# A graph attention layer and a mixture of experts: both scores of a node in layer 2's table rows, and the sort's features in two halves

## The chip, the cores and the metric

The kernel runs on one core of a Trainium2 chip. The metric is device time in microseconds, the median of several runs. The engines are named as in the profile: PE multiplies matrices (PEld is its loading of weights), DVE works on vectors, ACT evaluates functions and copies, POOL issues indirect DMAs (gathers and scatters by a list of indices), and SP issues plain DMAs. SP and ACT each have a queue of their own, and every engine runs its instructions in the order written.

## The reference

There are 6250 nodes with 256 features and 206250 edges (100000 pairs in both directions, and a loop at each node). The layer norm of x goes through eight attention heads of 64 features, then through one output layer of 256, then through a mixture of eight experts of which each node takes two.

```python
def _gat_layer(x, src, dst, W, b, a, g, beta, N, concat):
    h = x @ W.T + b
    d = W.shape[0]
    s_src = h @ a[:d]
    s_dst = h @ a[d:]
    score = s_src[src] + s_dst[dst]
    e = jnp.exp(-jax.nn.leaky_relu(score, ALPHA))
    h_prime = jax.ops.segment_sum(e[:, None] * h[dst], src, num_segments=N)
    # layer norm with g and beta, then elu (heads only)
...
heads = [_gat_layer(embeds, src, dst, W_heads[i], ...) for i in range(H)]
x = jnp.concatenate(heads, axis=1)
out = _gat_layer(x, src, dst, W_out, b_out, a_out, g_out, beta_out, N, concat=False)
return jax.nn.elu(out)
...
x = x + gnn(layernorm(x))
x = x + moe(layernorm(x))
```

A node thus has two scores per head: one as a source of an edge (s_src) and one as its destination (s_dst). An edge needs the source's score of one node, and the features and the destination's score of the other.

## The kernel before

The nodes lie in 49 blocks of 128. The work has three stages.

**The sort.** All edges are sorted by the block of their source, in 23 segments. A segment goes through stages on DVE and PE (`rows_of_blocks`, `counts_before`, `places_before`, `places`, `both_sides`) and ends in `append`: PE collects what each block gets (`run_ps`, L278), ACT copies it (L281), and POOL sends it out with four scatters (L283) into the list `srt` in DRAM. A scatter writes where another has written, so each waits until the one before has landed. Between these stages, by a schedule written out by hand, `tick` does the features of layer 1, a block at a time: `normed_x` (ACT), `turned_x` (PE), `turned_copy` (ACT), `products` (PE) and `table_rows`. `products` (L357 to L364) multiplies a block of 128 nodes with the weights `wt`, which have C1 = 528 columns: 512 features, then 8 scores as destination and 8 as source. It writes the 512 features to the PSUM bank `ph` and the 16 scores to the bank `pk`. The 256 input features are two pieces of 128 (KF = 2), and each such f32 product shows as two instructions in the profile; the bias is one more product, in bf16. `table_rows` copies both banks into one row of 528 and stores 520 columns of it to layer 1's table `tab1`; the source's scores stay in SBUF (`s1`) and are written to `ssrc1` once, at the end of the sort.

**Layers 1 and 2, `edges`.** Each block has at most 34 tiles of 128 edges, in groups of five. A group is loaded, weighted and added in stages at fixed distances: `sources` (SP, L643) loads the sources' numbers, `gather` (POOL, L649) fetches for each edge of a tile the table row of its destination, one gather a tile; `one_hot` (DVE), `source_sums` (PE, L662) and `weigh` (DVE and ACT, L665) make the weights of the edges; `messages` (DVE) makes the one-hot matrix and in layer 1 the weighted rows; `add` (PE, L705) sums them into the block's nodes. The source's score comes not from a table but from `sel`, made from the scores in SBUF. Edges that did not fit a block's tiles go through `far_messages`, one tile of at most 128 for each layer: it gathers the sources' scores from `ssrc` (L624) and the rows of the destinations (L626).

After each block of layer 1, `middle` does the layer norm, the elu and the products of layer 2, and stores a row for each node. That row has 258 columns: 256 features, the score as destination, the score as source. Its first R2 = 257 columns go to the table `tab2` (L845), the last one alone to `ssrc2` (L847), 4 bytes a node, and to `s2` in SBUF (L848).

After each block of layer 2, `tail` makes the tokens, and `experts` runs in between (L1019, L1027, L1032).

**A way out.** If the sort overflows, `every_edge` does all edges one by one. It stands behind a condition on `over_i`, and none of its instructions are in this trace.

Of the kernel before, what the change touches and what calls it, by code (L numbers as in the profile page):

```python
# [23 lines left out]
F32 = mybir.dt.float32  # L24
# [7 lines left out]
P = 128  # L32
# [16 lines left out]
def kernel(ctx: ExitStack, tc: tile.TileContext, x, src, dst, w_heads, b_heads, a_heads,  # L49
                        g_heads, beta_heads, w_out, b_out, a_out, g_out, beta_out, router, w1, b1, w2, b2,  # L50
                        out):
    nc = tc.nc
    N, F = x.shape
    E = src.shape[0]
    H, D = b_heads.shape
    HD = H * D
    R1 = HD + H
    R2 = F + 1
    NE = w1.shape[0]
    KF = F // P  # L60
    KH = HD // P
# [1 line left out]
    NB = -(-N // P)  # L63
    LAST = N - (NB - 1) * P
    EP = P - 1
# [21 lines left out]
    dram = ctx.enter_context(tc.tile_pool(name="dram", bufs=1, space=bass.MemoryType.DRAM))  # L87
# [2 lines left out]
    srow = dram.tile([NB * PIT], BF16, name="srow")  # L90
    tab1 = dram.tile([NB * P + 1, R1], F32, name="tab1")
    ssrc1 = dram.tile([NB * P, H], F32, name="ssrc1")
    ssrc2 = dram.tile([NB * P, 1], F32, name="ssrc2")
    tab2 = dram.tile([NB * P + 1, R2], F32, name="tab2")

    const = ctx.enter_context(tc.tile_pool(name="const", bufs=1))
# [192 lines left out]
    C1 = HD + 2 * H  # L289
# [67 lines left out]
    def products(b):  # L357
        ph = bank("ph", "ph")
        pk = bank("pk", "pk")
        for to, cols in ((ph, slice(0, HD)), (pk[:, :2 * H], slice(HD, C1))):  # L360
            for k in range(KF):
                nc.tensor.matmul(to, blocks[b][:, k, :], wt[:, k, cols], start=(k == 0), stop=False)
            nc.tensor.matmul(to, three, bias3[:, cols], start=False, stop=True)
        blocks[b] = ph, pk  # L364

    def table_rows(b):
        ph, pk = blocks.pop(b)
        row = sw.tile([P, C1], F32, name="row", bufs=2)
        nc.scalar.copy(row[:, HD:], pk[:, :2 * H])
        nc.scalar.copy(row[:, :HD], ph)  # L370
        nc.scalar.copy(s1[:, b, :], row[:, R1:])
        nc.sync.dma_start(tab1[b * P:(b + 1) * P, :], row[:, :R1])

# [213 lines left out]
    def edges(es, layer, table, sel, ssrc, k, width, block_done, more=None):  # L587

        row = width + k
        GB = 6 if k > 1 else 8
        RB = 6
        eb = es.enter_context(tc.tile_pool(name=f"edge_b{layer}", bufs=1))
# [23 lines left out]
        def far_messages():  # L618

            if layer == 1:  # L620
                yield from read_far(eb)
                yield
            ss = eb.tile([P, k], F32, name="far_ss")
            nc.gpsimd.indirect_dma_start(out=ss, out_offset=None, in_=ssrc,  # L624
                                         in_offset=bass.IndirectOffsetOnAxis(ap=far_src, axis=0))
            nc.gpsimd.indirect_dma_start(out=far_gt, out_offset=None, in_=table,  # L626
                                         in_offset=bass.IndirectOffsetOnAxis(ap=far_dst, axis=0))
            yield
            yield
            yield  # L630
            nc.vector.tensor_scalar_mul(ss, ss, far_good)
            nc.vector.tensor_add(ss, ss, far_gt[:, width:])
            edge_weights(eb, far_ee, ss)
            yield
            if k > 1:
                hv = far_gt[:, :width].rearrange("p (h d) -> p h d", h=k)
                nc.vector.tensor_mul(hv, hv, far_ee[:, :, None].to_broadcast([P, k, width // k]))
# [27 lines left out]
        def weigh(n):  # L665
            nt = size(n)
            ssum = eb.tile([P, GT, k], F32, name="ssum", bufs=2)[:, :nt]
            nc.vector.tensor_reduce(ssum, now[n]["ps"][:, :nt * 3 * k].rearrange("p (j t k) -> p j k t", j=nt, t=3),  # L668
                                    axis=AX.X, op=OP.add)
            nc.vector.tensor_add(ssum, ssum, now[n]["gt"][:, :nt, width:])  # L670
            if k > 1:
                ee = now[n]["ee"] = bank("ee", "ee")[:, :nt * k].rearrange("p (j k) -> p j k", j=nt)
            else:
                ee = tile_of(n, "ee", [P, GT, k], 3)[:, :nt]
            edge_weights(eb, ee, ssum)
# [62 lines left out]

    def every_edge(es, layer, table, ssrc, k, width):

        row = width + k
        rows = NB * P
        EP = 125
        EC = E // EP
        assert EP * EC == E
        gd = es.enter_context(tc.tile_pool(name=f"any_d{layer}", bufs=1, space=bass.MemoryType.DRAM))
        gc = es.enter_context(tc.tile_pool(name=f"any_c{layer}", bufs=1))
        gw = es.enter_context(tc.tile_pool(name=f"any_w{layer}", bufs=1))
        sums = gd.tile([rows + P, width], F32, name=f"sums{layer}")
        zeros = gc.tile([P, width], F32, name="zeros")  # L750
        nc.vector.memset(zeros, 0.0)
        for b in range(NB + 1):
            nc.sync.dma_start(sums[b * P:(b + 1) * P, :], zeros)
        lower = gc.tile([P, P], F32, name="lower")
        nc.vector.tensor_scalar(lower, iota_n, iota_p, None, op0=OP.is_lt)
        with tc.For_i(0, EC, 1) as i:
            si = gw.tile([EP, 1], I32, name="si")
            nc.sync.dma_start(si, src.rearrange("(p c) -> p c", p=EP)[:, bass.ds(i, 1)])
            di = gw.tile([EP, 1], I32, name="di")
            nc.sync.dma_start(di, dst.rearrange("(p c) -> p c", p=EP)[:, bass.ds(i, 1)])  # L760
            gt = gw.tile([EP, row], F32, name="gt_any")
            nc.gpsimd.indirect_dma_start(out=gt, out_offset=None, in_=table,
                                         in_offset=bass.IndirectOffsetOnAxis(ap=di, axis=0))
            sg = gw.tile([EP, k], F32, name="sg")
            nc.gpsimd.indirect_dma_start(out=sg, out_offset=None, in_=ssrc,
                                         in_offset=bass.IndirectOffsetOnAxis(ap=si, axis=0))
            nc.vector.tensor_add(sg, sg, gt[:, width:])
            ee = gw.tile([EP, k], F32, name="ee_any")
            edge_weights(gw, ee, sg)
            hv = gt[:, :width].rearrange("p (h d) -> p h d", h=k)  # L770
            nc.vector.tensor_mul(hv, hv, ee[:, :, None].to_broadcast([EP, k, width // k]))

            sf = gw.tile([EP, 1], F32, name="sf")
            nc.vector.tensor_copy(sf, si)
            wide = gw.tile([EP, P], F32, name="wide")
            nc.vector.tensor_copy(wide, sf.to_broadcast([EP, P]))
            pt = bank("pt", "pt_any")
            nc.tensor.transpose(pt[:, :EP], wide, ident[:EP, :EP])
            same = gw.tile([EP, EP], F32, name="same")
            nc.vector.tensor_scalar(same, pt[:EP, :EP], sf, None, op0=OP.is_equal)  # L780
            prev = gw.tile([EP, EP], F32, name="prev")
            nc.vector.tensor_mul(prev, same, lower[:EP, :EP])
            many = gw.tile([EP, 1], F32, name="many")
            nc.vector.tensor_reduce(many, prev, axis=AX.X, op=OP.max)

            to = gw.tile([EP, 1], F32, name="to")
            nc.vector.tensor_scalar(to, iota_p[:EP], float(rows), sf, op0=OP.add, op1=OP.subtract)
            nc.vector.scalar_tensor_tensor(to, to, many, sf, op0=OP.mult, op1=OP.add)
            ti = gw.tile([EP, 1], I32, name="ti")
            nc.vector.tensor_copy(ti, to)  # L790
            acc = bank("acc", "acc_any")
            nc.tensor.matmul(acc[:EP, :width], same, gt[:, :width], start=True, stop=True)
            old = gw.tile([EP, width], F32, name="old")
            nc.gpsimd.indirect_dma_start(out=old, out_offset=None, in_=sums,
                                         in_offset=bass.IndirectOffsetOnAxis(ap=ti, axis=0))
            nc.vector.tensor_add(old, old, acc[:EP, :width])
            nc.gpsimd.indirect_dma_start(out=sums, out_offset=bass.IndirectOffsetOnAxis(ap=ti, axis=0),
                                         in_=old, in_offset=None)
        return sums


    def middle(ms):
        mw = ms.enter_context(tc.tile_pool(name="mid_w", bufs=2))

        def block_done(b, acc):
# [36 lines left out]
            yield  # L842
            row = mw.tile([P, C2], F32, name="row2")
            nc.vector.tensor_add(row, ph[:, :C2], bo)
            nc.sync.dma_start(tab2[b * P:(b + 1) * P, :], row[:, :R2])  # L845
            with nc.allow_non_contiguous_dma(reason="one element of a node"):
                nc.sync.dma_start(ssrc2[b * P:(b + 1) * P, :], row[:, R2:])  # L847
            nc.vector.tensor_copy(s2[:, b, :], row[:, R2:])  # L848
        return block_done


# [239 lines left out]
    with ExitStack() as es:  # L1091
        psum_of("second", es, acc=2, ps=2, ffn=3, pt=1)
        done, more = tail(es)
        edges(es, 2, tab2, sel2, ssrc2, 1, F, done, more)


    with tc.If(nc.values_load(over_i[:1, :1], min_val=0, max_val=1) > 0):
# [9 lines left out]
                    pass  # L1107
        with ExitStack() as es:
            psum_of("second_any", es, acc=1, pt=2, ffn=3)
            sums = every_edge(es, 2, tab2, ssrc2, 1, F)  # L1110
            done, more = tail(es)
            bw = es.enter_context(tc.tile_pool(name="back2", bufs=2))
            for b in range(NB):
# [47 lines left out]
```

## Time and profile before

| | |
|---|---|
| median of 3 runs | 5668.95 us (5641.82 to 5675.06) |
| the profiled execution, its own time | 5686.65 us |
| its span | 5684.9 us |
| mean granted clock of PE | 0.834 |

By stage, in us of busy time, read from the busy times of each engine in stretches of the span:

| stretch | what | PE | DVE | ACT | POOL | DMA share |
|---|---|---|---|---|---|---|
| 0 to 429 | sort and features | 342.69 | 372.85 | 96.94 | 178.68 | 0.21 |
| 429 to 3108 | layer 1 | 1944.62 | 1725.45 | 378.37 | 1600.21 | 0.70 |
| 3108 to 5550 | layer 2 with experts | 1771.68 | 1137.96 | 794.19 | 1611.89 | 0.45 |
| 5550 to 5685 | last experts | 116.95 | 52.48 | 40.19 | 0.00 | 0.04 |

The profile is of one execution. A line of its answers in order of time has the start in us, the duration in us, the engine, the line of the kernel, the operation, what it writes and reads, how many alike follow each other, and in brackets how long the engine was idle before and what ended that. A group's line has the busy time, the mean of one in ns, and the idle time before with its releasers. PE's matmuls overlap, so that one's duration is longer than the distance to the next; distances are read from the starts. The releaser is inferred, and where an instruction waits for several things it can be the wrong one.

### The profile page before, as it was taken

Reading aid. Unit: us, or ns where it says so; the run is one execution under the profiler, and the core shown is the slowest. Engines: PE = TensorE matmul, PEld = TensorE weight load, DVE = VectorE, ACT = ScalarE, POOL = GpSimd, SP = SyncE. Lnnn points to the kernel's source line nnn. Section 1 sums busy time; section 2 is a strip of 40 time slices with the busy share of each in tenths; the row PEclk is TensorE's granted clock in tenths of the full one; section 3 lists DMA queues with packets and bytes.
Section 4 is the critical chain, followed back from the end, with each engine's and each line's share of the span. In section 5 each row is a group of like instructions: output and inputs, shape, how many; then the busy total and the mean of one; then the engine's idle time right before and its main releaser. Section 6 shows DMA issues by size and latency. Waiting matters only on the chain.

```text
span 5684.9 us, 52631 instructions
## 1 busy us (share of the span) xinstructions
PE 4175.9 (73%) x16462; PEld 2477.2 (44%) x16462; DVE 3288.7 (58%) x8048; ACT 1309.7 (23%) x2440; POOL 3390.8 (60%) x3450
## 2 busy tenths in 40 slices
PE   5984777777777777777776447777778777777778
PEld 4762333333333333333333335555555555545556
DVE  9975666666666666666666334454444445444444
ACT  1220111111111111111111113333334333333433
POOL 3446656665666666666554666666666666666660
PEclk8996878888888888888778668888888888888989
DMA  2216767786677777777665544444444444444440
GB/s 69 66 51 186 196 187 188 195 210 182 195 192 186 201 190 194 190 195 191 184 189 141 141 118 111 122 119 113 119 122 112 121 120 120 113 119 122 112 112 14
DMA packets 378008, 825.33 MB, mean 145 GB/s; under 512 B 91759, under 2 KB 210779, under 8 KB 377718
## 3 DMA queue, kind: packets, MB, share of 16 engines
q0 software_dynamic: 216464, 665.03, 44.0%
q1 hardware_dynamic: 155868, 151.02, 9.5%
q10 hardware_dynamic: 5386, 5.83, 0.3%
q8 instruction: 131, 2.15, 0.2%
q14 instruction: 159, 1.30, 0.1%
HBM read 792.59 MB, written 28.99 MB: 145 GB/s over the span
## 4 chain that ended last, share of the span: by engine, by line
PE 35%; DVE 26%; issue 17%; another core or an unknown queue 12%; POOL 7%; DMA 2%; DVEq 0%; ACT 0%; POOLq 0%; ACTq 0%; SPq 0%
PE acc L705 18%; DVE msg L687 10%; POOL gt L649 7%; PE ph L1019 6%; PE py L1027 6%; DVE hot L684 2%; DMA gt<-tab,dst_idx 2%; DVE hot L693 1%; DVE ot L656 1%; PE run_ps L278 1%; PE ps L662 1%; DVE ssum L670 1%; DVE ssum L668 1%; DVE what L266 1%
## 5 line engine op out<-in xcount | busy, mean ns | idle before, releaser
L649 POOL DMA_INDIRECT gt<-tab,dst_idx x3324 | 3206.4, 965 | 1908.4 <-issue 923.3
L705 PE MATMUL acc<-msg,hot 128*128 128x512 f32 x3324 | 1711.6, 659 | 180.4 <-issue 178.6
L705 PE MATMUL acc<-gt,hot 128*128 128x256 f32 x3324 | 1004.0, 445 | 176.2 <-issue 167.8
L705 PEld LDWEIGHTS acc<-msg,hot 128*128 128x128 f32 x3324 | 666.4, 209 | 944.5 <-issue 942.9
L687 DVE TENSOR_TENSOR msg<-gt,ee 128x2560 f32<-128x2560 f32 (+1 forms) x342 | 935.2, 2735 | 0.0
L705 PEld LDWEIGHTS acc<-gt,hot 128*128 128x128 f32 x3324 | 697.7, 219 | 337.1 <-issue 230.5
L585 ACT ACTIVATE ee<-lr 128x40 f32<-128x40 f32 (+3 forms) x684 | 141.7, 207 | 2348.7 <-DVE lr L584 1250.0
L662 PE MATMUL ps<-sel,ot 128*128 128x24 bf16 (+1 forms) x3324 | 204.4, 171 | 649.7 <-issue 314.8
L693 DVE TENSOR_SCALAR hot<-iota_n,sloc,ee 128x128 f32<-128x128 f32 x1662 | 461.6, 357 | 330.9 <-remote 166.6
L684 DVE TENSOR_TENSOR hot<-iota_ps,sloc 128x640 f32<-128x640 f32 (+1 forms) x342 | 273.4, 799 | 603.8 <-remote 514.2
L662 PEld LDWEIGHTS <-ot 128*128 128x128 bf16 x3324 | 192.3, 100 | 945.5 <-issue 707.0
L1032 DVE SCALAR_TENSOR_TENSOR xq<-py,comb,xq 128x256 f32<-128x256 f32 x392 | 171.0, 478 | 577.2 <-remote 162.5
L1027 PE MATMUL py<-w2s,h 128*128 128x256 f32 x1568 | 410.5, 402 | 57.9 <-issue 52.9
L1019 PE MATMUL ph<-tokt,w1s 128*128 128x512 f32 (+1 forms) x832 | 408.0, 618 | 25.1 <-issue 23.6
L585 ACT ACT_TABLE_LOAD x252 | 323.3, 1283 | 375.8 <-DVE lr L584 178.6
L1027 PEld LDWEIGHTS py<-w2s,h 128*128 128x128 f32 x1568 | 312.2, 203 | 149.9 <-issue 99.9
L283 POOL DMA_INDIRECT srt<-run,to x92 | 168.4, 1830 | 247.9 <-DMA srt<-run,to 148.8
L668 DVE TENSOR_REDUCE ssum<-ps 128x40 f32<-128x120 f32 (+3 forms) x684 | 149.6, 219 | 252.8 <-remote 197.4
L656 DVE TENSOR_SCALAR ot<-rb,iota_p 128x640 bf16<-128x640 bf16 (+1 forms) x684 | 259.0, 379 | 7.2 <-DMA rb<-srow 7.2
L1019 PEld LDWEIGHTS ph<-tokt,w1s 128*128 128x128 f32 x832 | 162.4, 206 | 168.1 <-issue 157.9
L1021 ACT ACTIVATE h<-ph,b1s 128x512 f32<-128x512 f32 (+1 forms) x208 | 135.5, 662 | 368.1 <-remote 210.1
L840 PE MATMUL ph<-wo,ht 128*128 128x258 f32 x392 | 126.1, 476 | 84.8 <-DVE ht L837 79.1
(248 smaller groups left out, 3248.6 us busy)
## 6 DMA issues: line engine op xcount, KB each, us to landing
rb<-srow SPq DMA_DIRECT2D x588, 160.0 KB
gt<-tab,dst_idx POOLq DMA_INDIRECT x3324
tab<-row SPq DMA_DIRECT2D x49, 260.0 KB
rb<-srow SPq DMA_DIRECT2D x96, 128.0 KB
tab<-row SPq DMA_DIRECT2D x49, 128.5 KB
xq<-in_x_dram SPq DMA_DIRECT2D x12, 512.0 KB
out_dram<-xq SPq DMA_DIRECT2D x12, 512.0 KB
xc<-in_x_dram SPq DMA_DIRECT2D x6, 896.0 KB
```

The costliest lines, as they stand in the source:

```text
L585: nc.scalar.activation(ee, lr, AF.Exp, scale=-1.0)
L649: nc.gpsimd.indirect_dma_start(out=gt[:, j, :], out_offset=None, in_=table, in_offset=bass.IndirectOffsetOnAxis(ap=dst_idx[c][:, t0 + j:t0 ...
L656: nc.vector.tensor_scalar(ot[:, :cols], now[n]["rb"][:, :cols], iota_p, None, op0=OP.is_equal)
L662: nc.tensor.matmul(ps[:, j * 3 * k:(j + 1) * 3 * k], ot[:, j * P:(j + 1) * P], sel[:, groups[n][0]].rearrange("p t k -> p (t k)"), start=T ...
L668: nc.vector.tensor_reduce(ssum, now[n]["ps"][:, :nt * 3 * k].rearrange("p (j t k) -> p j k t", j=nt, t=3), axis=AX.X, op=OP.add)
L684: nc.vector.tensor_tensor(hot, iota_ps[:, None, :P].to_broadcast([P, nt, P]), sl[:, :, None].to_broadcast([P, nt, P]), op=OP.is_equal)
L687: nc.vector.tensor_mul(msg.rearrange("p j (h d) -> p j h d", h=k), gt[:, :, :width].rearrange("p j (h d) -> p j h d", h=k), ee[:, :, :, No ...
L693: nc.vector.tensor_scalar(hot[:, j, :], iota_n, sl[:, j:j + 1], ee[:, j, :], op0=OP.is_equal, op1=OP.mult)
L705: nc.tensor.matmul(accs[b][:, :width], now[n]["hot"][:, j, :], now[n]["msg"][:, j, :width], start=(g == 0 and j == 0), stop=False)
L1019: nc.tensor.matmul(ph[:, :W], w1s[:, e, k, f * P:(f + 1) * P], tokt[:, k, :W], start=(k == 0), stop=(k == KF - 1))
L1027: nc.tensor.matmul(py[:, (i - lo) * F:(i - lo + 1) * F], h1[:, k, i * P:(i + 1) * P], w2s[:, e, k, :], start=(k == 0), stop=(k == KF - 1))
L1032: nc.vector.scalar_tensor_tensor(xq[:, i, :], py[:, (i - lo) * F:(i - lo + 1) * F], comb[:, i, e:e + 1], xq[:, i, :], op0=OP.mult, op1=OP.add)
```

## The change

- `tab2` gets a second score column: R2 is 258, and the row of a node is stored whole. `ssrc2` and its store of 4 bytes a node are gone. The gathers of layer 2 fetch the whole row of 258.
- `far_messages` of layer 2 (and `every_edge`) gather the source's score as part of a row of `tab2`, and use its last column.
- `products` splits the 528 columns as 264 and 264 instead of 512 and 16, and `table_rows` copies them so.

```diff
-    R2 = F + 1
+    R2 = F + 2
...
-    ssrc2 = dram.tile([NB * P, 1], F32, name="ssrc2")
...
     def products(b):
         ph = bank("ph", "ph")
         pk = bank("pk", "pk")
-        for to, cols in ((ph, slice(0, HD)), (pk[:, :2 * H], slice(HD, C1))):
+        for to, cols in ((ph[:, :C1 // 2], slice(0, C1 // 2)), (pk[:, :C1 // 2], slice(C1 // 2, C1))):
...
         row = sw.tile([P, C1], F32, name="row", bufs=2)
-        nc.scalar.copy(row[:, HD:], pk[:, :2 * H])
-        nc.scalar.copy(row[:, :HD], ph)
+        nc.scalar.copy(row[:, :C1 // 2], ph[:, :C1 // 2])
+        nc.scalar.copy(row[:, C1 // 2:], pk[:, :C1 // 2])
...
-        row = width + k
+        row = table.shape[1]
...
-            ss = eb.tile([P, k], F32, name="far_ss")
-            nc.gpsimd.indirect_dma_start(out=ss, out_offset=None, in_=ssrc,
+            got = eb.tile([P, ssrc.shape[1]], F32, name="far_ss")
+            ss = got[:, ssrc.shape[1] - k:]
+            nc.gpsimd.indirect_dma_start(out=got, out_offset=None, in_=ssrc,
...
-            nc.vector.tensor_add(ss, ss, far_gt[:, width:])
+            nc.vector.tensor_add(ss, ss, far_gt[:, width:width + k])
...
-            nc.vector.tensor_add(ssum, ssum, now[n]["gt"][:, :nt, width:])
+            nc.vector.tensor_add(ssum, ssum, now[n]["gt"][:, :nt, width:width + k])
...
             row = mw.tile([P, C2], F32, name="row2")
             nc.vector.tensor_add(row, ph[:, :C2], bo)
-            nc.sync.dma_start(tab2[b * P:(b + 1) * P, :], row[:, :R2])
-            with nc.allow_non_contiguous_dma(reason="one element of a node"):
-                nc.sync.dma_start(ssrc2[b * P:(b + 1) * P, :], row[:, R2:])
-            nc.vector.tensor_copy(s2[:, b, :], row[:, R2:])
+            nc.sync.dma_start(tab2[b * P:(b + 1) * P, :], row)
+            nc.vector.tensor_copy(s2[:, b, :], row[:, F + 1:])
...
-        edges(es, 2, tab2, sel2, ssrc2, 1, F, done, more)
+        edges(es, 2, tab2, sel2, tab2, 1, F, done, more)
```

More of the change, by code (lines that the diff above doesn't have):

```diff
@@ L739, in every_edge @@
     def every_edge(es, layer, table, ssrc, k, width):
-        row = width + k
+        row = table.shape[1]
         rows = NB * P
@@ L763, in every_edge @@
                                          in_offset=bass.IndirectOffsetOnAxis(ap=di, axis=0))
-            sg = gw.tile([EP, k], F32, name="sg")
-            nc.gpsimd.indirect_dma_start(out=sg, out_offset=None, in_=ssrc,
+            sr = gw.tile([EP, ssrc.shape[1]], F32, name="sr")
+            sg = sr[:, ssrc.shape[1] - k:]
+            nc.gpsimd.indirect_dma_start(out=sr, out_offset=None, in_=ssrc,
                                          in_offset=bass.IndirectOffsetOnAxis(ap=si, axis=0))
-            nc.vector.tensor_add(sg, sg, gt[:, width:])
+            nc.vector.tensor_add(sg, sg, gt[:, width:width + k])
             ee = gw.tile([EP, k], F32, name="ee_any")
@@ L1109 @@
             psum_of("second_any", es, acc=1, pt=2, ffn=3)
-            sums = every_edge(es, 2, tab2, ssrc2, 1, F)
+            sums = every_edge(es, 2, tab2, tab2, 1, F)
             done, more = tail(es)
```

## The prediction

> **What bounds the kernel now.** I read the page first, then the busy times by stage, then the instructions in order of time around each edit. The page's chain names no single owner of the span:
>
> ```profile
> span 5684.9 us, 52631 instructions
> ...
> PE 35%; DVE 26%; issue 17%; another core or an unknown queue 12%; POOL 7%; DMA 2%; DVEq 0%; ACT 0%; POOLq 0%; ACTq 0%; SPq 0%
> ```
>
> The edits lie in three stages: the sort (0 to 429 us), layer 1 (429 to 3108) and layer 2 (3108 to the end). In the sort the busy times by stage (PE, PEld, DVE, ACT, POOL, granted clock, DMA share, GB/s) are
>
> ```profile
> 250.00:330.00 80.00, 78.24 (x670) 61.42 (x670) 78.10 (x88) 21.98 (x72) 43.22 (x17) 0.98 0.19 63
> 330.00:390.00 60.00, 60.00 (x499) 46.16 (x497) 45.93 (x41) 17.13 (x56) 31.79 (x17) 1.00 0.15 50
> 390.00:430.00 40.00, 17.15 (x133) 13.60 (x130) 12.27 (x56) 3.33 (x12) 12.78 (x14) 0.74 0.15 31
> ```
>
> PE looks like the bound (60.00 of 60), and the edit of the products shortens PE. But the stage ends with the scatters, and POOL in order of time shows who is late:
>
> ```profile
> 394.82 0.96 POOL L283 DMA_INDIRECT srt<-run,to  x1 [2.01 <-DMA srt<-run,to]
> ...
> 405.71 0.95 POOL L283 DMA_INDIRECT srt<-run,to  x1 [3.64 <-DMA srt<-run,to]
> 408.72 0.96 POOL L283 DMA_INDIRECT srt<-run,to  x1 [2.06 <-DVE left L146]
> ...
> 426.35 0.95 POOL L283 DMA_INDIRECT srt<-run,to  x1 [1.51 <-DMA srt<-run,to]
> ```
>
> Each segment has four scatters, and each waits for the landing of the one before. The last segment's copy L281 runs at 402.85, yet its first scatter goes out at 419.05; the copy before it is at 392.33, its scatter at 408.72; the one before that at 379.90, its scatter at 394.82. The scatters run 15 to 16 us behind PE. The release "DVE left" at 408.72 is the trace's inference; the wait is the landing of the scatter of 405.71. So layer 1's first read of the sorted list (429.38) follows POOL's scatters, not PE.
>
> **The products in two halves.** One block on PE, in order of time:
>
> ```profile
> 263.22 1.88 PE L362 MATMUL ph<-wt,xt 128*128 128x512 f32 x4
> 264.94 0.38 PE L363 MATMUL ph<-bias,three 65*128 65x512 bf16 x1
> 265.16 0.52 PE L362 MATMUL pk<-wt,xt 128*128 128x16 f32 x4
> 265.52 0.17 PE L363 MATMUL pk<-bias,three 65*128 65x16 bf16 x1
> 265.55 0.42 PE L349 MATMUL pt<-ident,xn 128*128 128x128 f32 x2
> ```
>
> By the starts, a block takes 265.55 - 263.22 = 2.33 us: four pieces of 512 columns 1.72 (0.43 each), their bias 0.22, four pieces of 16 columns 0.36 (0.09 each, though 16 columns pro rata are 0.013), their bias 0.03. After it are eight pieces of 264 columns. The nearest row is L840's 128x258, where eight in a row at 3092.46 take 1.91 us; less the last one's tail (0.17, from 1.88 against 4 x 0.43 above) that is 0.218 each, so 0.223 for 264. Eight are 1.78, two biases 2 x 0.22 x 264/512 = 0.23, together 2.01. PE saves 0.32 us a block, 49 x 0.32 = 16 us in all.
>
> The page "TensorE: Matmul & The Clock Gate", section "Back-to-back issue gap", of the Trainium skill speaks against this edit: its sustained spacings (81 ns at 128 columns, 131 at 512) are linear with a fixed part, and by them two halves cost what 512 + 16 cost, so an estimate from it is a saving of 0. L705's 128x512 and L840's 128x258 here are proportional (0.43 and 0.218), so the trace decides.
>
> How much of the 16 us reaches the end? Until 330 DVE is 98% busy (78.10 of 80), so a faster PE only waits for it. From 330 on PE would lead, but the scatters lag by 15 us, and an earlier copy only waits longer. The one place where a scatter may wait for its data late in the stage is 244.62, behind the copy at 243.88; that copy stood behind L333, which waited 10.16 us for DVE, not PE. A scatter costs 0.95 us to issue where DVE is idle (after 405) and up to 4.62 us beside DVE's passes (L283: 953/1728/4620 ns). DVE's work stays the same, so finishing some us sooner only moves its idle time: from the 101.75 scatter on, 83 steps take 324.6 us (3.91 each), the last seven 2.52 each. I take -1 us, with bounds -16 (all of it on the path) and +5 (two scatters pushed from 2.5 to 4.7 us, the mean step between 250 and 330).
>
> ACT copies 264 + 264 instead of 512 + 16 columns: L370 takes 592 ns, L369 173, so 0.845 ns a column over a fixed part, 382 ns for each half, 764 against 765: nil.
>
> **The stores of 4 bytes.** Out go 49 issues on SP (L847, 425 ns, together 21 us) and their 128 pieces each. What is queued behind them on SP is L643's loads of rb, which wait for DVE to free a buffer (1294 us in total, SP's own waits), so the 21 us hide there; without that cover they would be 21. On the DMA engines I look at the last block, where nothing else moves, in 40 slices of 0.07 us from 3108.2 on:
>
> ```profile
> DMA  0026999953530000000000009977007665594748
> GB/s 0 0 88 220 382 338 338 309 162 46 4 2 0 0 0 0 0 0 0 0 0 0 0 0 37 55 18 18 0 0 18 18 18 18 18 37 55 110 128 128
> ```
>
> The table's 128 KB pass at 300 GB/s and more; the three slices after (46, 4, 2 GB/s) are the 4-byte pieces: 0.21 us. 49 x 0.21 = 10 us, with 0.3 us as upper end 15, all in layer 1. There DMA is busy 70%, and DMA with "unknown queue", where I count gathers that land late, is 2 + 12 = 14% of the chain: 0.14 x 10 = 1.4 us, taken as -2. Bounds 0 and -15. "DMA: Bandwidth & Descriptors", section "Bandwidth", gives 0.68 us for a DMA of 4 KB as the floor of its pieces; by that figure the estimate would be 49 x 0.68 = 33 us of DMA and -5 us. The 0.21 of this trace is used.
>
> At the end of layer 1 the first gather of layer 2 (3114.76) is released by the landing of rb, issued at 3108.99 when DVE's L149 ends, not by the store: -0.2 us at most, left out. DVE's copy of s2 stays; SP's store of the row grows from 1028 to 1032 bytes a node, nil.
>
> **The gathers of layer 2.** 1662 gathers fetch 1032 bytes a row instead of 1028. L649 in 500 to 3000 us, with rows of 2080 bytes, has a median of 949 ns, in layer 2 with 1028 also 949; the gap to the next is 0.30 in both. The issue doesn't see the row's length. DMA in layer 2 is 45% busy, and 0.4% more of it is nil while other limits hold. DVE and PE read the rows of gt at a pitch of 1032 bytes: L705 runs ten pieces of 256 columns in 2.27 us at full clock (0.21 each at pitch 1028), like L840 at 0.218 for 258, so the pitch of 1028 costs PE nothing that 1032 could give back. Bounds: the means by stage, 961 (layer 1) and 969 (layer 2) ns, differ by 8, call it 10, so 1662 x 0.010 = 17 us either way. Taken: 0. The one gather far_ss now brings 1032 bytes a row: it lands in 3.31 us and DVE then waits 1.09 more for far_gt, whose rows are as long, so nil.
>
> **Sum.** -1 - 2 + 0 = -3 us: the profiled execution's 5686.65 becomes 5684. That execution is 17.7 us (0.3%) over the median of 5668.95, so the median becomes 5666. The three runs span 33 us; 1%, 57 us, is about what a measurement of this kernel can tell from no change.
>
> **Rivals.**
> - PE's saving reaches the end and the stores were on the path. For it: PE 60.00 of 60 and its place in the chain. Against: the scatters' lag. -16 - 15: 5638.
> - Faster by over 1%: the 4-byte stores hold up gathers behind them by much more than they occupy. It needs 57/49 = 1.2 us each, against 0.21 seen. With 1.5 us, 5595.
> - Slower: the longer row costs each gather of layer 2, in POOL's issue or in the landing that the buffers wait for. At 10 ns it is +17 (5686); above 57/1662 = 34 ns it passes 1%. For it: POOL is busy 66% there, with 0.3 more us lost per gather, so each ns counts nearly in full. Against: 2080 and 1028 bytes have the same 949.
> - That the change leaves the stores in some other form is out: the two scores lie next to each other in the row that is stored anyway.
>
> **How the numbers follow.** Forecast, within 17 us of 5666: 0.55. First rival 0.25, second 0.06, third 0.14, of which 0.06 over 1%. Range 5632 (the first rival's 5638 with a few us of scatter between runs) to 5690 (the third at 10 ns with as much); outside lie the second rival and the third above that, about 0.15. Faster by over 1% 0.06, slower 0.06, within 1% 0.88.
>
> **What would show it.** Right: L362 has eight pieces of 0.22 us a block and PE is idle more between 330 and 400, while the last scatter stays at 426 (within 3 us) and its lag behind the last L281 grows to some 20 us; no L847; layer 1 as long within 10 us; L649 at 949 ns in layer 2. Wrong: the last scatter 8 us earlier or more (the first rival), layer 1 shorter by over 20 us (the second), L649 or its waits in layer 2 longer (the third).

## The result, and the profile after

On the chip of the comparison the changed kernel takes 5679.35 us (median of 20 runs, 5660.92 to 5697.71) and the kernel before 5664.60 (20 runs, 5637.00 to 5689.52): a ratio of 1.0027, interval 1.0014 to 1.0040. The forecast was -3 us; it came out 15 us the other way, and the whole interval lies above 1, so that this is a small loss and not no change. The time lies in the range that was given, the sign does not fit the forecast.

The profiled execution of the changed kernel took 5660.92 us, the shortest of its runs, and that of the kernel before 5686.65, one of its longest. The two spans (5659.2 and 5684.9) thus say the opposite of the medians, and only stages and single steps can be compared in them. The page, span and chain:

```profile
span 5659.2 us, 52576 instructions
...
PE 37%; DVE 24%; issue 16%; another core or an unknown queue 13%; POOL 9%; DMA 2%; DVEq 0%; ACT 0%; POOLq 0%; SPq 0%; ACTq 0%
```

The chain is as mixed as before; it shows no new owner. The same stretches of the sort by busy time (length, then PE, PEld, DVE, ACT, POOL with their instructions, granted clock, DMA share, GB/s):

```profile
250.00:330.00 80.00, 80.00 (x730) 70.38 (x729) 78.77 (x89) 23.55 (x73) 42.48 (x19) 1.00 0.20 65
330.00:390.00 60.00, 60.00 (x513) 51.54 (x512) 46.26 (x47) 20.90 (x66) 30.00 (x17) 1.00 0.17 59
390.00:430.00 40.00, 9.78 (x71) 7.85 (x68) 13.38 (x59) 0.44 (x1) 11.48 (x12) 0.59 0.12 19
```

Between 390 and 430 PE has 71 instructions left where it had 133: it finishes earlier. One block of the features on PE, in order of time:

```profile
262.92 1.05 PE L361 MATMUL ph<-wt,xt 128*128 128x264 f32 x4
263.81 0.28 PE L362 MATMUL ph<-bias,three 65*128 65x264 bf16 x1
263.93 1.05 PE L361 MATMUL pk<-wt,xt 128*128 128x264 f32 x4
264.82 0.28 PE L362 MATMUL pk<-bias,three 65*128 65x264 bf16 x1
264.94 0.38 PE L348 MATMUL pt<-ident,xn 128*128 128x128 f32 x2
```

From start to start a block takes 264.94 - 262.92 = 2.02 us, against 2.33 before. The sort's last copy is now at 394.50 (402.85 before), and POOL in order of time shows what becomes of it:

```profile
403.30 1.00 POOL L282 DMA_INDIRECT srt<-run,to  x1 [2.06 <-DVE pr L405]
...
413.62 0.96 POOL L282 DMA_INDIRECT srt<-run,to  x1 [2.04 <-DMA srt<-run,to]
...
420.92 0.95 POOL L282 DMA_INDIRECT srt<-run,to  x1 [1.51 <-DMA srt<-run,to]
```

The last segment's first scatter goes out 19.1 us behind its copy (413.62 - 394.50) where it was 16.2, so 8.4 us earlier on PE are 5.4 us at the last scatter (426.35 before).

The surprise is in layer 1, behind each store of a block's row. In the kernel before, one of the 4-byte stores is issued at 1621.53. Here are its stretches of 2 us (length, POOL's busy time with its instructions, granted clock, DMA share, GB/s):

```profile
1623.00:1625.00 2.00, 1.65 (x2) 0.92 0.97 336
1625.00:1627.00 2.00, 1.44 (x2) 0.50 1.99 152
1627.00:1629.00 2.00, 1.41 (x2) 0.73 0.69 25
1629.00:1631.00 2.00, 1.68 (x2) 1.00 0.52 52
1631.00:1633.00 2.00, 1.16 (x2) 1.00 0.53 98
1633.00:1635.00 2.00, 1.48 (x2) 1.00 0.97 373
```

In the changed kernel, where a row's store is issued at 1616.36, the same view:

```profile
1620.00:1622.00 2.00, 1.39 (x3) 1.00 0.94 312
1622.00:1624.00 2.00, 1.63 (x2) 1.00 0.89 256
1624.00:1626.00 2.00, 1.45 (x2) 1.00 0.73 215
1626.00:1628.00 2.00, 1.39 (x3) 1.00 0.82 189
```

POOL goes on issuing gathers in both, but in the kernel before little moves for some 6 us (25 to 98 GB/s between 1627 and 1633), and then the late gathers come at 373 GB/s. The DMA engines are not idle in this time: between 1625 and 1627 the packets that begin take 1.99 times what all 16 engines have, so that it is single packets that take long. Averaged over 30 row stores between 600 and 2500 us, the traffic in the 1-us slices from 4 to 12 us after the row's store is, in GB/s:

```
before         231  74  46  49  60  72  86 182
changed        237 189 186 165 174 221 188 217
```

The packets of these traces say what is slow. The 4-byte pieces themselves pass in 9 ns each. But the gathers' packets of 4160 bytes (two rows) that begin 5 to 11 us after one of these 30 row stores take 845 ns on average, against 230 in the changed kernel, and there are 2772 of them against 7316. So a store of 128 pieces of 4 bytes holds up the gathers for some 6 us, where the forecast counted the 0.21 us in which its pieces pass.

The quiet place that the forecast looked at, the end of layer 1, shows the same. The DMA view of the changed kernel, in slices of 0.07 us from 0.63 us after the last row's store, as the one in the forecast:

```profile
DMA  0027999850000000000000000232242432544685
GB/s 0 0 88 251 354 354 354 295 177 15 0 0 0 0 0 0 0 0 0 0 0 0 0 0 0 73 128 110 110 146 73 146 110 91 128 128 146 165 256 183
```

The last 16 slices hold the first loads of rb for layer 2. Here they move at 125 GB/s on average, with the engines mostly two to five tenths busy; in the forecast's view at 42 GB/s, with the engines mostly four to nine tenths busy. The last row's store and the first gather of layer 2, before and then after:

```profile
3107.57 0.32 SPq L845 DMA_DIRECT2D tab<-row  x1
3114.76 0.95 POOL L649 DMA_INDIRECT gt<-tab,dst_idx  x1 [51.78 <-DMA rb<-srow]
...
3086.13 0.32 SPq L846 DMA_DIRECT2D tab<-row  x1
3089.42 0.94 POOL L649 DMA_INDIRECT gt<-tab,dst_idx  x1 [45.62 <-DMA rb<-srow]
```

The gather comes 7.19 us behind the store before and 3.29 after; it is 4.0 to 10.4 us in the eight profiles of this case that have the stores of 128 4-byte pieces, 3.0 to 3.8 in the twelve that don't.

Within layer 1 of this chip hardly anybody waits for the hold-up: between 500 and 2500 us POOL waits 10.8 us in all for a landed gather before and 6.5 after. That the change takes this hold-up away and is still slower here is what the experiments are about.

### The profile page after: what moved, and what is told of

It is laid out like the page before. It is cut to its first block, busy times and chain, and to the rows that moved or that the text cites. A ratio compares the mean times of both kernels' runs of the same rounds, so it can differ in the third digit from the quotient of the medians.

```text
span 5659.2 us, 52576 instructions
## 1 busy us (share of the span) xinstructions
PE 4175.6 (74%) x16462; PEld 2501.3 (44%) x16462; DVE 3287.9 (58%) x8048; ACT 1313.3 (23%) x2440; POOL 3379.3 (60%) x3450
## 4 chain that ended last, share of the span: by engine, by line
PE 37%; DVE 24%; issue 16%; another core or an unknown queue 13%; POOL 9%; DMA 2%; DVEq 0%; ACT 0%; POOLq 0%; SPq 0%; ACTq 0%
PE acc L705 19%; DVE msg L687 8%; POOL gt L649 8%; PE ph L1018 6%; PE py L1026 6%; DVE hot L693 2%; DVE hot L684 1%; DVE ot L656 1%; DMA gt<-tab,dst_idx 1%; PE run_ps L277 1%; PE ps L662 1%; DVE ssum L668 1%; DVE ssum L670 1%; DVE what L265 1%
## 5 line engine op out<-in xcount | busy, mean ns | idle before, releaser
L649 POOL DMA_INDIRECT gt<-tab,dst_idx x3324 | 3194.7, 961 | 1897.4 <-issue 922.8
L687 DVE TENSOR_TENSOR msg<-gt,ee 128x2560 f32<-128x2560 f32 (+1 forms) x342 | 935.2, 2735 | 0.0
L684 DVE TENSOR_TENSOR hot<-iota_ps,sloc 128x640 f32<-128x640 f32 (+1 forms) x342 | 273.4, 799 | 572.5 <-remote 433.1
```

The lines of the kernel that those rows point to most:

```text
L649: nc.gpsimd.indirect_dma_start(out=gt[:, j, :], out_offset=None, in_=table, in_offset=bass.IndirectOffsetOnAxis(ap=dst_idx[c][:, t0 + j:t0 ...
L684: nc.vector.tensor_tensor(hot, iota_ps[:, None, :P].to_broadcast([P, nt, P]), sl[:, :, None].to_broadcast([P, nt, P]), op=OP.is_equal)
L687: nc.vector.tensor_mul(msg.rearrange("p j (h d) -> p j h d", h=k), gt[:, :, :width].rearrange("p j (h d) -> p j h d", h=k), ee[:, :, :, No ...
```

## The experiments

They ran in sets, each on one chip with its own runs of the kernel before. With the comparison above, the sets turned out to be of two sorts: the kernel before took 5602, 5624 and 5665 us in three of them (called slow chips here and in the expectations), and 4862, 4892 and 4899 us in the other three (fast chips). It is the same program; what makes a chip one or the other is not known. All ratios are against the kernel before of the same set.

**First set, kernel before 5601.83 us: one part at a time.** The halves alone:

```diff
-        for to, cols in ((ph, slice(0, HD)), (pk[:, :2 * H], slice(HD, C1))):
+        for to, cols in ((ph[:, :C1 // 2], slice(0, C1 // 2)), (pk[:, :C1 // 2], slice(C1 // 2, C1))):
...
-        nc.scalar.copy(row[:, HD:], pk[:, :2 * H])
-        nc.scalar.copy(row[:, :HD], ph)
+        nc.scalar.copy(row[:, :C1 // 2], ph[:, :C1 // 2])
+        nc.scalar.copy(row[:, C1 // 2:], pk[:, :C1 // 2])
```

> Only the products in two halves; rows, stores and gathers as before. The change measured +0.27% (some +15 us), while its one profiled execution ends the scatters 5.4 us earlier. Theory 'halves' (the 15 us come from the sort's edit, by what it leaves behind): +15 us, 1.0027. Theory 'row' (they come from layer 2's row of 258 columns) and theory 'stores' (from the missing 49 stores): -5 us, 0.999, the scatters' last issue at about 421 instead of 426, layers 1 and 2 as before.

Measured: 5600.03 us, ratio 0.9988 (0.9967 to 1.0009).

The stores alone: the 4-byte stores go, and the scores are written to `ssrc2` once, behind layer 1.

```diff
-            with nc.allow_non_contiguous_dma(reason="one element of a node"):
-                nc.sync.dma_start(ssrc2[b * P:(b + 1) * P, :], row[:, R2:])
...
+        with nc.allow_non_contiguous_dma(reason="one element of a node"):
+            nc.sync.dma_start(ssrc2.rearrange("(b p) h -> p b h", p=P), s2)
         pieces(es.enter_context(tc.tile_pool(name="sel2", bufs=1)), sel2, s2, 1)
```

> Only the 49 stores of 4 bytes a node are gone; layer 2's far edges read the sources' scores from one store of s2 at the end of layer 1. Rows and products as before. Theory 'stores': +15 us, 1.0027, in layer 1, where the 49 issues stood in SP's queue. Theory 'row' and theory 'halves': 0 to -2 us.

Measured: 5657.30 us, 1.0077 (1.0049 to 1.0104).

The longer row alone: R2 = F + 2, stored and gathered whole, while the 4-byte stores stay.

```diff
-    R2 = F + 1
+    R2 = F + 2
...
-            nc.sync.dma_start(tab2[b * P:(b + 1) * P, :], row[:, :R2])
+            nc.sync.dma_start(tab2[b * P:(b + 1) * P, :], row)
             with nc.allow_non_contiguous_dma(reason="one element of a node"):
-                nc.sync.dma_start(ssrc2[b * P:(b + 1) * P, :], row[:, R2:])
+                nc.sync.dma_start(ssrc2[b * P:(b + 1) * P, :], row[:, F + 1:])
```

> Only the row: 258 columns stored whole and gathered whole in layer 2; the 49 stores of 4 bytes and the products as before. Theory 'row': +15 to +20 us, 1.003, all of it in layer 2 (between its first gather and the end), some 10 ns for each of the 1662 gathers. Theory 'stores' and theory 'halves': 0.

Measured: 5601.67 us, 1.0001 (0.9978 to 1.0025).

The change without the halves (`products` and `table_rows` as before):

> The change without the products in two halves. Theory 'row': +15 to +20 us as the row alone. Theory 'stores': +15 as the stores alone. Theory 'halves': 0. If the row alone and the stores alone are both 0 and this is +20, it is what the two do together: the wide far_ss tile, which moves the tiles of layer 2 that are laid out after it by 1028 bytes.

Measured: 5639.40 us, 1.0068 (1.0044 to 1.0092). Both runs that drop the stores lose, and the two that keep them don't: the loss comes with the stores. It lies in layer 1, from the first gather to the last row's store: 2604.5 (halves) and 2606.9 (row) us with the stores, 2658.6 (stores) and 2636.7 (change without halves) without.

**Second set, kernel before 4899.21 us: number of transfers or number of pieces?** Dropping the stores takes 49 transfers off SP's queue and 128 pieces with each. One store of one piece put back, on top of the run without the stores:

```diff
+    few = dram.tile([NB, 1], F32, name="few")
...
+            nc.sync.dma_start(few[b:b + 1, :], row[:1, R2:])
             nc.vector.tensor_copy(s2[:, b, :], row[:, R2:])
```

> As s_only (no 4-byte store of the 128 nodes, 1.0077 there), but SP issues in its place one store of a single 4-byte element a block, so that the number of SP's DMAs and their turn over the completion counters is that of the kernel before, and the 128 pieces are missing. Theory 'count' (what slowed s_only is one DMA less a block on SP, by its issue of 0.4 us or by which counter the next loads get): 1.000. Theory 'pieces' (what helps is the 128 small packets on the DMA rings themselves): 1.007 as s_only.

Measured: 4822.46 us, 0.9847 (0.9830 to 0.9864).

The row's store in two parts of 128 and 129 columns, on top of the run without the stores:

```diff
-            nc.sync.dma_start(tab2[b * P:(b + 1) * P, :], row[:, :R2])
+            nc.sync.dma_start(tab2[b * P:(b + 1) * P, :P], row[:, :P])
+            nc.sync.dma_start(tab2[b * P:(b + 1) * P, P:], row[:, P:R2])
```

> As s_only, but the row of 257 columns is stored as two DMAs, 128 and 129 columns: two DMAs a block as before, on all 16 engines, each with pieces of 512 bytes and more. Theory 'count': 1.000. Theory 'pieces': 1.007, since no piece is small.

Measured: 4824.45 us, 0.9847 (0.9830 to 0.9863).

The kernel before with each 4-byte store made twice:

```diff
                 nc.sync.dma_start(ssrc2[b * P:(b + 1) * P, :], row[:, R2:])
+                nc.sync.dma_start(twice[b * P:(b + 1) * P, :], row[:, R2:])
```

> The kernel before with its store of 4 bytes a node issued twice a block, the second to a place that nothing reads. Theory 'pieces': faster still, 0.993 if it goes on in proportion, 1.000 if one store is enough. Theory 'count': not settled by the count alone (10 DMAs a block instead of 9), 1.000 to 1.007. The sum in the prediction (10 us of DMA a store) would give 1.001.

Measured: 4913.20 us, 1.0028 (1.0017 to 1.0039). (The 10 us in this expectation are those of all 49 stores, not of one.)

The 4-byte stores issued by ACT, one step of the schedule later:

```diff
-            with nc.allow_non_contiguous_dma(reason="one element of a node"):
-                nc.sync.dma_start(ssrc2[b * P:(b + 1) * P, :], row[:, R2:])
             nc.vector.tensor_copy(s2[:, b, :], row[:, R2:])
+            yield
+            with nc.allow_non_contiguous_dma(reason="one element of a node"):
+                nc.scalar.dma_start(ssrc2[b * P:(b + 1) * P, :], row[:, R2:])
```

> The kernel before with its 4-byte stores issued from ACT one step later instead of from SP: the 128 pieces stay, SP's queue is that of s_only. Theory 'pieces': 1.000 (0 to +0.2% for ACT's 49 issues). If it is SP's own queue that matters (0.4 us between the store of the row and the next load of rb): 1.007 as s_only.

Measured: 4883.10 us, 0.9964 (0.9954 to 0.9974). The hold-up moves with the store: averaged as above, the traffic is at 38 to 46 GB/s from 8 to 13 us after the row's store. Why this is 0.4% faster than the kernel before is not known. With 49 transfers of one piece, or 49 more of 128 pieces of 512 bytes and more, the time is the same and 1.5% below the kernel before; so on this chip the 128 pieces of 4 bytes are the cost. Whether that is by the size of a piece, or because the 128 pieces land side by side within 512 bytes of `ssrc2`, no run separates. The sign had turned with the chip, so the set could not say whether the count of transfers makes the loss on the slow ones. A second copy of the store adds little because it lies in the same hold-up: averaged as above, the traffic stays under 80 GB/s from 5 to 12 us after the row's store (read from the run with zeros and each store twice, below), with one copy (the run with zeros alone) from 5 to 11.

**Third set, kernel before 5623.81 us: the same question on a slow chip.** The whole change:

> The whole change once more, beside three of its neighbours on one chip. Theory 'chip' (what sets layer 1's pace differs from chip to chip: where the kernel before takes about 5600 to 5670 us it is matrix instructions that TensorE issues late, and dropping the stores lengthens layer 1; where it takes about 4900 us it is the gathers' pace on POOL, and dropping them shortens it): about 1.003 to 1.007 of the kernel before on a chip of the first sort, about 0.98 to 0.985 on one of the second, with the run copies' end 8 us earlier on both. Theory 'count' (the number of transfers on SP's queue, which the change lowers by 49, decides): 1.003 or slower on any chip.

Measured: 5631.38 us, 1.0020 (1.0005 to 1.0035). The stores alone:

> Left out as in the earlier run: the 49 stores of 4 bytes a row; the scores go to their table once, behind layer 1. Theory 'chip': 1.005 to 1.010 where the kernel before takes about 5600 us or more, 0.982 to 0.988 where it takes about 4900 us. Theory 'count': 1.005 to 1.010 on any chip, since here SP's queue has 49 transfers fewer and nothing put back.

Measured: 5653.69 us, 1.0052 (1.0034 to 1.0070). With one piece put back:

> As the run without the stores, with one store of a single 4-byte piece in the place of each one of 128 pieces, so that SP's queue holds as many transfers as before. Theory 'chip': within 0.003 of the run without the stores that is beside it, on any chip. Theory 'count': 0.985 of the kernel before on a fast chip and at most 1.000 on a slow one, 0.007 or more below the run without the stores that is beside it.

Measured: 5649.25 us, 1.0047 (1.0032 to 1.0062). With each store twice:

> The kernel before with each store of 4-byte pieces made twice, the second to a table that nothing reads. Theory 'chip': 0.990 to 1.000 where the kernel before takes about 5600 us or more (the pieces hold the gathers back and so spread the work that TensorE gets), 1.002 to 1.004 where it takes about 4900 us. Theory 'count': within 0.002 of 1.000, or the 0.7% that dropping a transfer cost, gained once more.

Measured: 5610.21 us, 0.9970 (0.9957 to 0.9982). One piece a block costs what none costs (1.0047 and 1.0052), so theory 'count' is out on the slow chip, as it was on the fast one. And doubling the pieces turns its sign too: a gain of 0.3% here, a loss of 0.3% there.

The runs without the stores and with one piece overstate the loss somewhat, by an edit of mine: the single store of all scores behind layer 1. Layer 2 takes 2561 us in both runs of this set and 2548 in the changed kernel; POOL stands for some 12 us at its start, behind its first eight gathers (11.90 us behind the gather of 3109.53 in the run without the stores; the run with each store twice has no such stop there). The change itself has no such store, and neither has the change without the halves, which lost 0.7% in the first set.

**What only the slow chips show.** In the run without the stores of the third set, PE's chosen lines in order of time, with one each of DVE and POOL:

```profile
1058.65 0.20 PE L662 MATMUL ps<-sel,ot 128*128 128x24 bf16 x2 [1.24 <-issue]
...
1060.39 0.17 PE L662 MATMUL ps<-sel,ot 128*128 128x24 bf16 x1 [1.55 <-issue]
...
1063.21 0.18 PE L662 MATMUL ps<-sel,ot 128*128 128x24 bf16 x1 [2.64 <-issue]
...
1065.30 0.18 PE L662 MATMUL ps<-sel,ot 128*128 128x24 bf16 x1 [1.91 <-issue]
...
1070.26 0.69 DVE L684 TENSOR_TENSOR hot<-iota_ps,sloc 128x512 f32<-128x512 f32 x1 [11.19 <-remote]
...
1073.41 1.04 POOL L649 DMA_INDIRECT gt<-tab,dst_idx  x1 [7.27 <-DVE far_hot L697]
```

PE issues products of 0.2 us some 2 us apart, and nothing that the trace shows holds it ("issue"). DVE runs out of buffers and stands 11 us, POOL behind it 7. The busy times of the same stretch (PE, PEld, DVE, ACT, POOL, granted clock, DMA share, GB/s):

```profile
1054.00:1058.00 4.00, 3.40 (x8) 1.24 (x7) 2.57 (x2) 0.00 (x0) 3.08 (x4) 1.00 0.88 276
1058.00:1062.00 4.00, 0.37 (x3) 0.12 (x2) 0.68 (x3) 0.21 (x1) 3.09 (x4) 0.96 0.82 234
1062.00:1066.00 4.00, 0.36 (x2) 0.21 (x2) 0.00 (x0) 0.00 (x0) 3.08 (x4) 0.50 0.81 219
```

The clock is still granted in full when these gaps begin and is at 0.50 behind the first two, so here it does not start them. I counted such groups in layer 1 (gaps over 0.6 us put down to "issue", at most 6 us apart, over 1.5 us together): 57 to 68 in each of the ten profiles from slow chips, about three gaps in some 7 us each, with 289 to 384 us of gaps in all, and none in the ten profiles from fast chips. Over a group's first gap the clock is 0.89 to 0.96 on average, in the 4 us from its last one's end 0.53 to 0.59. In the change of the third set the gaps are 376 us, of the 528 by which its layer 1 (2660.6) is longer than that of the change on a fast chip (2132.4, below).

**Fourth set, kernel before 4891.64 us: zeros in layer 1's features.** To tell whether these gaps come from the electrical load of PE's data ('load') or from late instructions ('supply'), the 512 feature columns of layer 1's rows were written as zeros, so that layer 1's sums are not those of the reference; the scores, and so the weights of layer 1 and the sorted list, stay.

```diff
-        nc.scalar.copy(row[:, :HD], ph)
+        nc.scalar.activation(row[:, :HD], ph, AF.Identity, scale=0.0)
```

> The kernel before with the 512 feature columns of layer 1's table rows written as zeros (scale 0 in the copy), the scores and everything else as before: TensorE's messages in layer 1 are zeros, its instructions the same. In the slow chips' traces some 60 to 70 times in layer 1 TensorE issues single matrix instructions about 2 us apart for some 10 us, with nothing to wait for, while the granted clock is still 1.0. Theory 'load' (TensorE is held because of the electrical load of what it computes): without the load the gaps are gone, layer 1 falls from about 2620 to about 2200 us, the ratio to the kernel before is 0.90 to 0.94 on a slow chip, near 1.00 on a fast one, which has no gaps. Theory 'supply' (instructions or semaphores arrive late, whatever the data): 0.99 to 1.01 on any chip and as many gaps.

Measured: 4894.07 us, 1.0007 (0.9997 to 1.0017). The set fell on a fast chip, where there are no gaps to take away: nothing follows for load against supply. It does show that on this chip the data make no difference to the time, so that the next runs stand for the real ones. Without the stores:

> The same zeros, and the 49 stores of 4 bytes a row left out (scores to their table once, behind layer 1). If the gaps are what makes the loss of the stores cost time, then without gaps this is 70 to 90 us faster than the run with zeros alone, as on the fast chip. If the stores' absence costs time by itself, it is 20 to 40 us slower than that run.

Measured: 4817.39 us, 0.9854 (0.9839 to 0.9869). The change:

> The whole change with the same zeros in layer 1's features. By theory 'load' 75 to 100 us faster than the run with zeros alone (the stores' 70 to 90 us and some 8 us of the sort); by theory 'supply' 10 to 20 us slower than it on a slow chip.

Measured: 4794.83 us, 0.9803 (0.9790 to 0.9817). Each store twice:

> The same zeros, and each store of 4-byte pieces made twice. By theory 'load' 10 to 20 us slower than the run with zeros alone (as on the fast chip, +14 us), where with the real data on a slow chip it was 14 us faster than the kernel before. By theory 'supply' 10 to 20 us faster.

Measured: 4904.18 us, 1.0029 (1.0018 to 1.0040).

**Fifth set, kernel before 4861.66 us: zeros and the real change, once more.**

> The whole change with the 512 feature columns of layer 1's rows written as zeros, once more. On a fast chip 0.980 of the kernel before, as it was. On a slow chip, theory 'load' (TensorE is held back by the electrical load of what it computes): no gaps in layer 1, layer 1 at the fast chip's 2110 to 2140 us where the change with its real data takes about 2650, layer 2 as before (its data are not zeros), together 0.89 to 0.92 of the kernel before. Theory 'supply' (instructions or semaphores come late, whatever the data): 1.000 to 1.006, as many gaps as with the real data.

Measured: 4795.44 us, 0.9862 (0.9841 to 0.9883).

> The whole change with its real data, beside the one with zeros. On a fast chip 0.978 to 0.983 of the kernel before (zeros alone were worth nothing there, 1.0007), on a slow one 1.001 to 1.005 with 60 to 70 groups of gaps in layer 1.

Measured: 4798.34 us, 0.9869 (0.9848 to 0.9891). A fast chip again, so load against supply stays open; but the change with its real data is 63 us faster than the kernel before on it.

The two sides of this are in the waits. In the run with zeros and all stores (which stands for the kernel before on a fast chip, 1.0007), between 500 and 2500 us (us in total, times, longest):

```profile
POOL gt L649 <- DMA gt<-tab,dst_idx: 110.0, 122, 4.1
...
DVE ssum L670 <- DMA gt<-tab,dst_idx: 388.8, 123, 8.6
```

In the change on a fast chip, the same stretch:

```profile
POOL gt L649 <- DMA gt<-tab,dst_idx: 24.4, 80, 0.3
...
DVE ssum L670 <- DMA gt<-tab,dst_idx: 323.6, 214, 3.7
```

The long waits, up to 8.6 us on DVE and 4.1 on POOL, are gone with the stores; the run with zeros and without the stores, on the chip of the first of these two, says the same (21.3 us in all on POOL, 316.4 on DVE). With them gone, POOL issues its gathers at 0.95 + 0.30 us without a break, 1662 x 1.25 = 2078 us, and layer 1 takes 2132. By stage, in us, one execution each:

| | sort's last scatter | layer 1 | layer 2 |
|---|---|---|---|
| before, slow chip (5665) | 426.4 | 2671.9 | 2577.3 |
| change, slow chip (5665) | 420.9 | 2655.8 | 2573.1 |
| change, slow chip (5624) | 424.2 | 2660.6 | 2547.6 |
| each store twice, slow chip (5624) | 422.0 | 2628.5 | 2551.1 |
| zeros, stores kept, fast chip (4892) | 433.1 | 2212.8 | 2235.9 |
| zeros, stores gone, fast chip (4892) | 427.4 | 2129.4 | 2250.3 |
| each store twice, real data, fast chip (4899) | 427.3 | 2224.8 | 2235.5 |
| one piece instead, real data, fast chip (4899) | 424.6 | 2132.6 | 2248.6 |
| change, real data, fast chip (4862) | 421.0 | 2132.4 | 2233.0 |

The first two rows are the profiled executions of the result; their layer 1 contradicts the medians, as their spans do. On one and the same fast chip dropping the stores thus saves (2212.8 - 2129.4) / 49 = 1.7 us for each store of layer 1.

## Why the prediction was wrong

**The products in two halves: right.** 2.02 us a block against 2.01 forecast, and what that rests on, that eight pieces of 264 cost 0.22 each, is in the lines above. By the estimate that was weighed there from the two sustained spacings of the Trainium skill ("TensorE: Matmul & The Clock Gate", "Back-to-back issue gap"), a block would have stayed at 2.33; the row was right to decide.

**What of it reaches the end: right mechanism, small size off.** The scatters do end the sort, but in the profiled execution their lag took up only 3 us of the 8 that PE's part ended earlier. The last scatter of six profiled executions with the halves is at 423.6 us on average (420.0 to 429.3), of fourteen without at 428.3 (421.4 to 433.1): about -5 us where -1 was taken. The two ranges overlap, and the latest of the six is that of the halves alone (429.3), whose time, 0.9988, cannot tell -1 from -5 either.

**The stores of 4 bytes: this step failed.** "DMA is busy 70%, and DMA with 'unknown queue' ... is 14% of the chain: 0.14 x 10 = 1.4 us, taken as -2. Bounds 0 and -15." Two things were wrong, the price and the bound.

The price, 0.21 us, is the time in which the pieces themselves pass. It was read at the end of layer 1, "where nothing else moves", but the loads of rb move there next, and the forecast's own view has them: behind its 0.21 us the engines are busy and move 42 GB/s. The first gather of layer 2, which was put down to rb alone with "-0.2 us at most", came 3.9 us sooner behind the row's store (3.29 against 7.19). In the midst of the gathers the hold-up is some 6 us, of which 1.7 us a store reach the end of layer 1 on a fast chip. The 0.68 us that "DMA: Bandwidth & Descriptors" of the Trainium skill, section "Bandwidth", gives for a transfer of its own would have been too small as well. The forecast's second rival named this mechanism (1.2 us each from which it decides) and had a chance of 0.06, because only the pieces were priced; the trace of before had the answer 49 times, in the GB/s behind any store. On the fast chips that rival is what happened (0.9869 for the whole change, 0.9803 with zeros in the features), on the chip of the comparison it is not.

The bound of 0 excluded a loss without a reason, and on the slow chips dropping the stores does cost: 1.0068 (38 us) for the change without halves, 1.0020 and 1.0027 for the whole. This is the sign that the forecast missed. That the time still lay in the range is luck: the range's upper end was made for the third rival, the gathers' longer row, which did not happen.

**SP's queue: right.** With 49 issues put back the time stays what it was without them: one piece a block on both sorts of chip (1.0047 beside 1.0052, and 0.9847 beside 0.9854 on another fast chip), the row in two on the fast one (0.9847).

**The gathers' longer row: right.** 1.0001 for the row alone, with its interval within 14 us, and L649's median is 946 ns, against 949. The third rival is out.

**Why the sign turns, and what stays open.** On fast chips it is shown: the hold-up makes POOL and DVE wait, and the gathers' pace sets layer 1. On slow chips the same hold-up is in the traffic, yet POOL waits for the gathers' landing only 10.8 to 27.3 us in the four profiles with the stores and 3.0 to 6.5 in the six without, against 110.0 and 21.3 on the fast chip. In the profiles of the result it waits most for DVE's `messages` (L687, 317.4 us before and 378.5 after), and DVE in its turn stands in PE's gaps as in the lines above. So PE's gaps seem to set the pace there, and the hold-up passes behind them. That explains a gain of nothing, not a loss. The loss itself (0.2 to 0.7%) goes with the 4-byte pieces, in the dose too, since doubling them gains 0.3%. A candidate is that pauses in the gathers spread PE's work and spare it some gaps: their sum is 289, 330, 350 and 358 us in the four profiles from slow chips with the stores, 335 to 384 in the six without. The two groups overlap, and it is not shown. The granted clock over layer 1 does not part them either (0.823 to 0.843 with the stores, 0.823 to 0.835 without). Nor is it whether the gaps come from load or supply: both runs with zeros that were to tell fell on chips without gaps.

## What to carry to other kernels

The price of a transfer is not the time in which its own bytes pass: look at what the other traffic does in the microseconds after it, averaged over all its issues, beside a stretch without it, and do not stop at the slice in which its last piece went. A transfer that stalls others costs only where somebody waits for those others, so ask in each stage what sets its pace, and whether that is the same on the chips that the kernel will meet. A bound that excludes a loss needs a reason as much as one that includes a gain.

## What the hardware showed unexpectedly

- The same program takes 4862 to 4899 us on some chips and 5602 to 5665 on others, all of it in layers 1 and 2 (2132 and 2656 us of layer 1 in the change); the sort is alike.
- A store of 128 pieces of 4 bytes from 128 partitions lowers the traffic beside gathers from about 200 to 40 to 90 GB/s for some 6 us, while a store of 128 pieces of 512 bytes or more does nothing of the kind. Its own pieces pass in 9 ns each; the gathers' packets behind them take 845 ns on average where they take 230 without it.
- On slow chips PE issues single products some 2 us apart, about three in 7 us, about every 40 us of layer 1, and in most groups the granted clock falls only behind the first of these gaps.
- Zeros in the features of layer 1 change nothing on a fast chip (1.0007).
